# Layer 1's state-space scan in half-chunk steps with two channel groups

## The chip, the core and the metric

The kernel runs on one core of a Trainium2 chip. Its engines work side by side: TensorE (PE in the profile, with its weight loads as PEld), VectorE (DVE), ScalarE (ACT), GpSimd (POOL) and SyncE (SP), which issues most of the DMA transfers. The metric is the time of one execution on the device, in microseconds, as the median of several runs. Everything is in fp32.

## What is computed

Four layers follow one another on an image of 2 x 64 channels x 96 x 96. Layer 0 is attention over the 9216 positions, layer 1 a small convolution and one state-space block ("Mamba"), layer 2 four such blocks (two directions along each of two axes), and layer 3 a dynamic 3 x 3 filter. The change touches the state-space block of layer 1. Cut to what matters:

```python
def _mamba(h, ...):                        # h: (batch, L = 9216, 64)
    ...                                    # projections, short convolution: xc, z (batch, L, 128)
    dt = softplus(dt @ dt_proj_w.T + dt_proj_b)       # (batch, L, 128)
    A = -exp(A_log)                                   # (128, 16)
    dA  = exp(dt[..., None] * A)                      # decay, per channel and state
    dBx = dt[..., None] * Bm[:, :, None, :] * xc[..., None]
    def step(hc, inp):
        dA_t, dBx_t, C_t = inp
        hc = hc * dA_t + dBx_t                        # the recurrence along L
        y = einsum('bds,bs->bd', hc, C_t)
        return hc, y
    _, ys = lax.scan(step, zeros, ...)
    ys = (ys + xc * Dp) * silu(z)
    return einsum('bld,cd->blc', ys, out_proj_w)
```

In layer 1 the recurrence runs over all 9216 positions of an image. In layer 2 it runs over single rows or columns of 96 positions and starts at zero in each.

## The kernel before

The sequence is cut into chunks of `CH = 768` positions, 12 to an image. A unit is one chunk: layer 1 has 24 units, layer 2 has 96. The 128 channels x 16 states are 2048 recurrences; 128 partitions hold 8 channels x 16 states, so a unit has 16 groups of 8 channels. For each unit, `dt` and `dt * xc` are written to DRAM and read back so that every channel's row lands on 16 partitions (the tile `spread`).

Layer 1 takes one channel group over the whole chunk in a step (768 columns). Layer 2 (`u.paired`) takes two channel groups over half a chunk, `HALF = 384` columns each, so it also has 16 steps of 768 columns; its sequences begin inside a chunk, where the decay is made zero, and one scan can run across both groups.

```python
def paired(self, step):
    half, m = divmod(step, self.STEPS // 2)
    return half, (2 * m, 2 * m + 1)

def read(self, u, step):                            # DMA: spread <- rows
    u.dtu[step] = self.work("spread", 2 * CH, bufs=6)
    if not u.paired:
        self.nc.sync.dma_start(out=u.dtu[step], in_=u.rows[8 * step : 8 * step + P])
        return
    half, groups = self.paired(step)
    for q, n in enumerate(groups):
        row = u.rows[8 * n : 8 * n + P, bass.ts(half, CH)]
        self.nc.sync.dma_start(out=u.dtu[step][:, bass.ts(q, CH)], in_=row)

def decay(self, u, step):                           # ScalarE: h = exp(rate * dt)
    h = u.h[step] = self.work("h", bufs=9)
    if not u.paired:
        self.nc.scalar.activation(h, u.dtu[step][:, :CH], AF.Exp, scale=u.w.rates[:, step : step + 1])
        return
    for q, n in enumerate(self.paired(step)[1]):
        dt = u.dtu[step][:, q * CH : q * CH + HALF]
        self.nc.scalar.activation(h[:, bass.ts(q, HALF)], dt, AF.Exp, scale=u.w.rates[:, n : n + 1])

def shared(self, u, half=0):                        # TensorE: B of the unit, into PSUM
    if u.paired:
        sides, halves = [self.low[0]], [half]
    else:
        (sides, u.B), halves = self.places[1], range(2)
    for j, p in zip(halves, sides):
        self.nc.tensor.matmul(p, lhsT=u.w.bc[0], rhs=u.xc[:, bass.ts(j, HALF)], start=True, stop=True)

def inputs(self, u, step):                          # VectorE: the product dt*x*B, into PSUM
    if not u.paired:
        u.bx = self.places[0][1]
        self.nc.vector.tensor_mul(u.bx, u.dtu[step][:, CH:], u.B)
        return
    bx = self.places[step % 2][1].rearrange("p (q t) -> p q t", q=2)
    x = u.dtu[step].rearrange("p (q a t) -> p q a t", q=2, a=2)[:, :, 1]
    B = self.low[0].unsqueeze(1).to_broadcast([P, 2, HALF])
    self.nc.vector.tensor_mul(bx, x, B)

def scan(self, u, step):                            # VectorE: the recurrence; GpSimd: times C
    nc = self.nc
    h = u.h[step]
    if not u.paired:
        first = u.carry[:, step : step + 1]
        nc.vector.tensor_tensor_scan(h, h, u.bx, first, ALU.mult, ALU.add)
        nc.gpsimd.tensor_copy(first, h[:, CH - 1 :])
        nc.gpsimd.tensor_mul(h, h, u.C)
        return
    bx = self.places[step % 2][1]
    way = slice(None, None, -1) if u.rev else slice(None)
    nc.vector.tensor_tensor_scan(h[:, way], h[:, way], bx[:, way], 0.0, ALU.mult, ALU.add)
    ...                                             # GpSimd: h times C, C broadcast over the two groups

def gather(self, u, step):                          # TensorE: sum over the 16 states, into y
    if u.paired:
        half, groups = self.paired(step)
        parts = [(half, self.low[1], q, n) for q, n in enumerate(groups)]
        ...
    else:
        parts = [(j, p, j, step) for j, p in enumerate(self.low)]
        ...
    ...                                             # first the direct term Dp * xc, then two products a step
```

PSUM is used as follows: `places` are two tiles of 768 columns, `low` two of 384. In layer 1 `places[0]` holds the product, `places[1]` holds B, and `low` the two halves of y. In layer 2 both `places` hold products in turn, `low[0]` holds B and `low[1]` y, each for half a chunk.

The order of the steps in the program, the same for all engines (each engine takes its own instructions out of it):

```python
for n in range(begin, len(steps) + end + 1):
    s = n % self.STEPS
    ...                                             # read of step n + 5, decay of step n + 3
    if at(n):
        u = at(n)[0]
        if not u.paired:
            self.inputs(u, s)
        elif s % 2 == 0:
            self.inputs(u, s)
            self.inputs(u, s + 1)
        self.scan(u, s)
        if u.paired and s == 6:
            self.shared(u, 1)
        if s == (14 if u.paired else 15) and unit(n // self.STEPS + 1):
            after = unit(n // self.STEPS + 1)
            if after.paired and not u.paired:       # from layer 1 to layer 2
                for late in (2, 1, 0):
                    self.gather(u, s - late)
                self.y_read(u)
                u.drained = True
            self.shared(after)
    ...                                             # gather of step n - 2; then the pieces of the units to come and past
```

The pieces are the other parts of a unit (norm, convolution, gate, step size, C, the output), spread over the steps of the units before and after; each uses one shared PSUM tile `mm` in turn.

Of the kernel before, what the change touches and what calls it, by code (L numbers as in the profile page):

```python
# [19 lines left out]
FP = mybir.dt.float32  # L20
AF = mybir.ActivationFunctionType
ALU = mybir.AluOpType
# [3 lines left out]
P = 128  # L26
B, C, H, W = 2, 64, 96, 96
L = H * W
EPS = 1e-5
NB = 512  # L30

D_STATE, DT_RANK, D_CONV = 16, 4, 4
HALF = 4 * W
CH = 2 * HALF
# [579 lines left out]
class Mamba:  # L614
# [19 lines left out]
    def __init__(self, k, tables, wk, dram, ps, ps_m):  # L634
        self.k, self.nc, self.t = k, k.nc, tables
        self.wk, self.dram, self.ps_m = wk, dram, ps_m


        self.places = [self.wide(ps.tile([P, 2 * NB], FP, name=f"place{i}")) for i in range(2)]
        self.low = [ps.tile([P, NB], FP, name=f"low{i}")[:, :HALF] for i in range(2)]  # L640

    def work(self, tag, n=CH, **kw):
        return self.wk.tile([P, n], FP, tag=tag, name=tag, **kw)
# [138 lines left out]
    def step_read(self, u):  # L782
        nc = self.nc

        u.both = self.work("dtu", 2 * CH, bufs=1)
        order = "p (j a t) -> p a j t" if u.paired else "p (a j t) -> p a j t"
        both = u.both.rearrange(order, a=2, j=2)
        u.dt, u.e = both[:, 0], both[:, 1]
        u.kept = self.by_half(self.work("kept", bufs=1))
        p = self.by_half(u.p)  # L790
        nc.scalar.activation(u.e, p, AF.Abs, bias=u.w.dt_b)
        nc.scalar.activation(u.dt, p, AF.Relu, bias=u.w.dt_b)
# [39 lines left out]

    def paired(self, step):
        half, m = divmod(step, self.STEPS // 2)
        return half, (2 * m, 2 * m + 1)

    def read(self, u, step):
        u.dtu[step] = self.work("spread", 2 * CH, bufs=6)  # L840
        if not u.paired:
            self.nc.sync.dma_start(out=u.dtu[step], in_=u.rows[8 * step : 8 * step + P])
            return
        half, groups = self.paired(step)
        for q, n in enumerate(groups):
            row = u.rows[8 * n : 8 * n + P, bass.ts(half, CH)]
            self.nc.sync.dma_start(out=u.dtu[step][:, bass.ts(q, CH)], in_=row)

    def decay(self, u, step):

        h = u.h[step] = self.work("h", bufs=9)
        if not u.paired:
            self.nc.scalar.activation(h, u.dtu[step][:, :CH], AF.Exp, scale=u.w.rates[:, step : step + 1])  # L853
            return
        for q, n in enumerate(self.paired(step)[1]):
            dt = u.dtu[step][:, q * CH : q * CH + HALF]
            self.nc.scalar.activation(h[:, bass.ts(q, HALF)], dt, AF.Exp, scale=u.w.rates[:, n : n + 1])  # L857

    def shared(self, u, half=0):

        if u.paired:
            sides, halves = [self.low[0]], [half]
        else:
            (sides, u.B), halves = self.places[1], range(2)
        for j, p in zip(halves, sides):
            self.nc.tensor.matmul(p, lhsT=u.w.bc[0], rhs=u.xc[:, bass.ts(j, HALF)], start=True, stop=True)  # L866

    def inputs(self, u, step):

        if not u.paired:  # L870
            u.bx = self.places[0][1]
            self.nc.vector.tensor_mul(u.bx, u.dtu[step][:, CH:], u.B)  # L872
            return
        bx = self.places[step % 2][1].rearrange("p (q t) -> p q t", q=2)
        x = u.dtu[step].rearrange("p (q a t) -> p q a t", q=2, a=2)[:, :, 1]
        B = self.low[0].unsqueeze(1).to_broadcast([P, 2, HALF])
        self.nc.vector.tensor_mul(bx, x, B)  # L877

    def scan(self, u, step):
        nc = self.nc  # L880
        h = u.h[step]
        if not u.paired:
            first = u.carry[:, step : step + 1]
            nc.vector.tensor_tensor_scan(h, h, u.bx, first, ALU.mult, ALU.add)  # L884
            nc.gpsimd.tensor_copy(first, h[:, CH - 1 :])  # L885
            nc.gpsimd.tensor_mul(h, h, u.C)  # L886
            return
        bx = self.places[step % 2][1]
        way = slice(None, None, -1) if u.rev else slice(None)
        nc.vector.tensor_tensor_scan(h[:, way], h[:, way], bx[:, way], 0.0, ALU.mult, ALU.add)  # L890
        h = h.rearrange("p (q t) -> p q t", q=2)
        C = u.C[:, bass.ts(self.paired(step)[0], HALF)]
        nc.gpsimd.tensor_mul(h, h, C.unsqueeze(1).to_broadcast([P, 2, HALF]))  # L893

    def gather(self, u, step):

        if u.paired:
            half, groups = self.paired(step)
            parts = [(half, self.low[1], q, n) for q, n in enumerate(groups)]
            begin, end = step % 8 == 0, step % 8 == 7  # L900
        else:
            parts = [(j, p, j, step) for j, p in enumerate(self.low)]
            begin, end = step == 0, step == self.STEPS - 1
        h = u.h[step]
        if begin:
            for half, p in {half: p for half, p, _, _ in parts}.items():
                self.nc.tensor.matmul(p, lhsT=u.w.direct, rhs=u.xc[:, bass.ts(half, HALF)], start=True, stop=False)  # L907
        for i, (_, p, q, n) in enumerate(parts):
            stop = end and (i == 1 or not u.paired)
            self.nc.tensor.matmul(p, lhsT=self.t.gather[n], rhs=h[:, bass.ts(q, HALF)], start=False, stop=stop)  # L910

    def y_half(self, u):
        if u.paired:
            u.y = self.work("yg")
            self.nc.scalar.copy(u.y[:, :HALF], self.low[1])  # L915

    def y_read(self, u):
        if u.paired:
            self.nc.scalar.copy(u.y[:, HALF:], self.low[1])
        elif not u.drained:  # L920
            u.y = self.work("yg")
            for j, p in enumerate(self.low):
                self.nc.scalar.copy(u.y[:, bass.ts(j, HALF)], p)

    def y_gate(self, u):
        self.nc.gpsimd.tensor_mul(u.y, u.y, u.gate)
# [60 lines left out]
    OTHER = (3, 5)  # L987

    @staticmethod
    def lates(now, s):  # L990
        halves = now and now[0].paired
        if s == 2 or (s == 10 and halves):
            return ()
        if s == 3 or (s == 11 and halves):
            return (3, 2)
        return (2,)

    def run(self, units, first, n_first, other):


        for u in units:
            u.dtu, u.h, u.paired, u.drained = {}, {}, not u.carry, False
        steps = [(u, s) for u in units for s in range(self.STEPS)]
        at = lambda n: steps[n] if 0 <= n < len(steps) else None
        reads = ("norm_square", "norm_root", "conv_read", "gate_read", "step_read", "c_read", "tail_read")

        table = [[] for _ in range(self.STEPS)]
        unit = lambda i: units[i] if i < len(units) else None
        for offset, name in self.PIECES:
            table[offset % self.STEPS].append((name not in reads, offset, name))  # L1010
        begin, end = self.PIECES[0][0], self.PIECES[-1][0]
# [13 lines left out]
        for n in range(begin, len(steps) + end + 1):  # L1025
            s = n % self.STEPS
            if at(n + self.READ):
                self.read(*at(n + self.READ))
            if at(n + self.DECAY):
                self.decay(*at(n + self.DECAY))  # L1030
            if at(n):
                u = at(n)[0]


                if not u.paired:
                    self.inputs(u, s)
                elif s % 2 == 0:
                    self.inputs(u, s)
                    self.inputs(u, s + 1)
                self.scan(u, s)  # L1040
                if u.paired and s == 6:
                    self.shared(u, 1)
                if s == (14 if u.paired else 15) and unit(n // self.STEPS + 1):
                    after = unit(n // self.STEPS + 1)
                    if after.paired and not u.paired:

                        for late in (2, 1, 0):
                            self.gather(u, s - late)
                        self.y_read(u)
                        u.drained = True  # L1050
                    self.shared(after)
            if n == -1:
                self.shared(units[0])

            for late in self.lates(at(n), s):
                if at(n - late) and not (at(n - late)[0].drained):
                    self.gather(*at(n - late))
            for late in (False, True):
                for is_late, offset, name in table[s]:
                    i = (n - offset) // self.STEPS  # L1060
                    if is_late == late and (0 if n >= 0 else 1) <= i < len(units):
                        getattr(self, name)(units[i])
                if s in self.OTHER and n >= 0 and not late:
                    next(other, None)
# [289 lines left out]
```

## Time and profile before

| | |
|---|---|
| median of 3 runs | 8185.35 us (8180.19 to 8186.09) |
| profiled execution, span | 8174.9 us |
| TensorE (PE) busy | 7554.5 us, 92% |
| VectorE (DVE) busy | 6785.6 us, 83% |
| ScalarE (ACT) busy | 5045.4 us, 62% |
| GpSimd (POOL) busy | 4755.1 us, 58% |
| DMA | 1725.90 MB, mean 211 GB/s |
| layer 1's products and scans | from 2752.4 to 3937.1 us |
| layer 2's products and scans | from 3942.3 to 8093.4 us |

A busy share is a mean over four layers with different limits, so it has to be read by stage. In lists of instructions, `L884` is a line of the kernel, "out<-in" names the tiles, "x2" says that two like instructions are merged into one line, and a bracket at the end gives the engine's idle time ahead of the instruction and what ended it. The clock is the share of its full speed that TensorE was granted.

### The profile page before, as it was taken

How to read it: one execution, taken by the hardware profiler on the slowest of the kernel's cores; microseconds unless marked ns; L12 is line 12 of the kernel's file. 1: busy time of each engine (PE TensorE's matmuls, PEld its weight loads, DVE VectorE, ACT ScalarE, POOL GpSimd, SP SyncE). 2: the span in 40 equal slices, each digit the busy share in tenths (PEclk: the TensorE clock that was granted, in tenths of full speed). 3: DMA queues.
4: the chain of work that ended last, by engine and by line, in shares of the span. 5: the costliest groups of instructions: out<-in, count | busy, mean ns of one | idle time of the engine just before them, and what ended most of it. 6: DMA issues, size and time to landing. Idle time of an engine off the chain costs nothing.

```text
span 8174.9 us, 80364 instructions
## 1 busy us (share of the span) xinstructions
PE 7554.5 (92%) x24578; PEld 3358.0 (41%) x24578; DVE 6785.6 (83%) x5136; ACT 5045.4 (62%) x6473; POOL 4755.1 (58%) x3146
## 2 busy tenths in 40 slices
PE   9999999999999799999889998989999999999897
PEld 3333333333333344444444444444444444444443
DVE  6666666666666599988899999999999999999999
ACT  4444444444444566665676677777777777777774
POOL 0000000000000588888888888898999989888895
PEclk9999999999999798988999999999999999999999
DMA  1000000000000588777888888888898888888885
GB/s 42 1 1 1 1 1 1 3 4 4 4 4 5 205 294 296 284 286 277 292 315 317 317 321 333 330 324 331 334 337 328 330 336 336 331 321 334 324 329 211
DMA packets 538496, 1725.90 MB, mean 211 GB/s; under 512 B 59844, under 2 KB 60996, under 8 KB 537544
## 3 DMA queue, kind: packets, MB, share of 16 engines
q1 hardware_dynamic: 536608, 1717.66, 56.8%
q8 instruction: 194, 3.18, 0.2%
q10 hardware_dynamic: 1448, 3.05, 0.1%
q14 instruction: 246, 2.02, 0.1%
HBM read 1522.68 MB, written 197.79 MB: 210 GB/s over the span
## 4 chain that ended last, share of the span: by engine, by line
PE 21%; POOL 13%; issue 12%; ACT 8%; DMA 8%; DVE 4%; SPq 0%; DVEq 0%; ACTq 0%; POOLq 0%
PE low L910 10%; DMA spread<-rows 6%; POOL h L886 5%; POOL h L893 4%; PE mm L666 4%; ACT h L857 4%; PE conv L754 4%; DVE place L877 2%; DMA rows<-dtu 1%; PE low L907 1%; PE conv L748 1%; DVE h L890 1%; POOL dtu L811 1%; PE low L866 1%; ACT raw L773 1%
## 5 line engine op out<-in xcount | busy, mean ns | idle before, releaser
L910 PE MATMUL low<-h,pair 128*128 128x384 f32 x7680 | 2865.4, 515 | 44.2 <-POOL h L886 26.5
L893 POOL TENSOR_TENSOR h<-h,C 128x768 f32<-128x768 f32 x1536 | 2755.1, 1819 | 231.7 <-DVE h L890 225.1
L890 DVE TENSOR_TENSOR_SCAN h<-h,place 128x768 f32<-128x768 f32 x1536 | 2604.3, 1737 | 4.9 <-ACT h L857 4.9
L910 PEld LDWEIGHTS low<-h,pair 128*128 128x128 f32 x7680 | 1503.2, 201 | 1288.6 <-issue 270.7
L307 ACT ACTIVATE e<-f_exp 128x1536 f32<-128x1536 f32 x864 | 1207.1, 1449 | 1223.7 <-PE f_exp L297 1223.7
L363 DVE TENSOR_TENSOR acc_e<-acc_e,e 128x1536 f32<-128x1536 f32 x792 | 1389.9, 1755 | 684.5 <-ACT e L307 645.2
L857 ACT ACTIVATE h<-spread,xa 128x384 f32<-128x384 f32 x3072 | 1717.2, 607 | 368.7 <-DMA spread<-rows 336.8
L877 DVE TENSOR_TENSOR place<-spread,low 128x768 f32<-128x768 f32 x1536 | 1388.3, 949 | 251.0 <-PE low L866 238.4
L336 POOL TENSOR_TENSOR xa<-xa,t_att 64x512 f32<-64x512 f32 x36 | 45.4, 1261 | 2612.4 <-ACT t_att L334 2612.4
L314 PE MATMUL y_att<-e,xb 128*64 128x512 f32 x5184 | 1243.6, 601 | 0.0
L297 PE MATMUL f_exp<-theta,phi 64*128 64x512 f32 x5184 | 1234.4, 606 | 1.0 <-DVE xb L280 0.5
L297 PEld LDWEIGHTS f_exp<-theta,phi 64*128 64x128 f32 x5184 | 466.2, 186 | 754.6 <-issue 460.8
L884 DVE TENSOR_TENSOR_SCAN h<-h,state,place 128x768 f32<-128x768 f32 x384 | 696.1, 1813 | 67.7 <-ACT h L853 19.2
L886 POOL TENSOR_TENSOR h<-h,C 128x768 f32<-128x768 f32 x384 | 695.3, 1811 | 31.4 <-POOL state L885 1.0
L314 PEld LDWEIGHTS y_att<-e,xb 128*64 128x64 f32 x5184 | 341.5, 136 | 830.7 <-issue 829.3
L765 ACT ACTIVATE raw<-conv,cols 128x768 f32<-128x768 f32 x120 | 108.2, 901 | 886.1 <-PE conv L754 587.0
L754 PE MATMUL conv<-xn,xa 64*128 64x384 f32 (+3 forms) x1536 | 557.9, 503 | 16.6 <-DVE xa L1128 5.3
L872 DVE TENSOR_TENSOR place<-spread,place 128x768 f32<-128x768 f32 x384 | 369.1, 961 | 129.3 <-PE place L866 116.9
L853 ACT ACTIVATE h<-spread,rates 128x768 f32<-128x768 f32 x384 | 351.1, 931 | 175.0 <-DMA spread<-rows 173.6
L907 PE MATMUL low<-raw,xa 128*128 128x384 f32 x384 | 220.2, 662 | 257.8 <-ACT yg L915 175.6
L754 PEld LDWEIGHTS conv<-xn,xa 64*128 64x128 f32 x1536 | 277.6, 190 | 286.7 <-issue 98.7
L805 POOL TENSOR_TENSOR kept<-dtu,kept 128x768 f32<-128x768 f32 x120 | 218.2, 1819 | 285.1 <-ACT kept L798 285.1
(207 smaller groups left out, 6041.4 us busy)
## 6 DMA issues: line engine op xcount, KB each, us to landing
spread<-rows SPq DMA_DIRECT2D x3072, 384.0 KB, 6.4
spread<-rows SPq DMA_DIRECT2D x384, 768.0 KB, 4.5
rows<-dtu SPq DMA_DIRECT2D x240, 768.0 KB, 5.8
image<-pre SPq DMA_DIRECT2D x11, 384.0 KB, 2.3
xb<-image SPq DMA_DIRECT2D x11, 384.0 KB, 7.9
xa<-in_x SPq DMA_DIRECT2D x1, 2304.0 KB, 22.2
out<-xa ACTq DMA_DIRECT2D x7, 240.0 KB, 2.0
out<-xa SPq DMA_DIRECT2D x1, 1200.0 KB
```

The source lines that it names most:

```text
L297: nc.tensor.matmul(fs[j // 3][:, bass.ts(j % 3, NB)], lhsT=phi[at, bass.ts(m // 2, P)], rhs=theta[at, bass.ts(i, NB)], start=True, stop=True,)
L307: nc.scalar.activation(e, f, AF.Exp)
L314: nc.tensor.matmul(y[rows_of(m % 2)], lhsT=g[:, m, :], rhs=es[j // 3][:, bass.ts(j % 3, NB)], start=m < 2, stop=m >= KEYS - 2,)
L363: nc.vector.tensor_add(acc, acc, e)
L754: self.nc.tensor.matmul(p3[:, :, o], lhsT=lhsT, rhs=x3[:, :, i], **flags)
L857: self.nc.scalar.activation(h[:, bass.ts(q, HALF)], dt, AF.Exp, scale=u.w.rates[:, n : n + 1])
L877: self.nc.vector.tensor_mul(bx, x, B)
L884: nc.vector.tensor_tensor_scan(h, h, u.bx, first, ALU.mult, ALU.add)
L886: nc.gpsimd.tensor_mul(h, h, u.C)
L890: nc.vector.tensor_tensor_scan(h[:, way], h[:, way], bx[:, way], 0.0, ALU.mult, ALU.add)
L893: nc.gpsimd.tensor_mul(h, h, C.unsqueeze(1).to_broadcast([P, 2, HALF]))
L910: self.nc.tensor.matmul(p, lhsT=self.t.gather[n], rhs=h[:, bass.ts(q, HALF)], start=False, stop=stop)
```

## The change

Layer 1 now uses the steps of layer 2: two channel groups over half a chunk. Its recurrence carries over from chunk to chunk, so one scan can't run across both groups; each step has two scans of 384 columns, each starting from the state that its group had after the half chunk before. The product of the next step comes ahead of the scans, into the other of two PSUM tiles, so that no scan has to wait for the product right in front of it and no product for the scan right in front of it. With one form of step, the branches for the two kinds and the drain between the layers go, and `low` becomes `B` and `y`.

```diff
-        self.low = [ps.tile([P, NB], FP, name=f"low{i}")[:, :HALF] for i in range(2)]
+        self.B, self.y = [ps.tile([P, NB], FP, name=name)[:, :HALF] for name in ("B", "y")]
...
     def read(self, u, step):
+        half, turns = self.turns(step)
         u.dtu[step] = self.work("spread", 2 * CH, bufs=6)
-        if not u.paired:
-            self.nc.sync.dma_start(out=u.dtu[step], in_=u.rows[8 * step : 8 * step + P])
-            return
-        half, groups = self.paired(step)
-        for q, n in enumerate(groups):
+        for q, n in enumerate(turns):
...
     def decay(self, u, step):
 
         h = u.h[step] = self.work("h", bufs=9)
-        if not u.paired:
-            self.nc.scalar.activation(h, u.dtu[step][:, :CH], AF.Exp, scale=u.w.rates[:, step : step + 1])
-            return
-        for q, n in enumerate(self.paired(step)[1]):
+        for q, n in enumerate(self.turns(step)[1]):
...
     def scan(self, u, step):
         nc = self.nc
-        h = u.h[step]
-        if not u.paired:
-            first = u.carry[:, step : step + 1]
-            nc.vector.tensor_tensor_scan(h, h, u.bx, first, ALU.mult, ALU.add)
-            nc.gpsimd.tensor_copy(first, h[:, CH - 1 :])
-            nc.gpsimd.tensor_mul(h, h, u.C)
-            return
...
+        half, turns = self.turns(step)
+        h, bx = u.h[step], self.places[step % 2][1]
+        h2 = h.rearrange("p (q t) -> p q t", q=2)
+        if u.carry:
+            state = u.carry[:, turns[0] : turns[1] + 1]
+            for q in range(2):
+                at = bass.ts(q, HALF)
+                nc.vector.tensor_tensor_scan(h[:, at], h[:, at], bx[:, at], state[:, q : q + 1], ALU.mult, ALU.add)
+            nc.gpsimd.tensor_copy(state.unsqueeze(2), h2[:, :, HALF - 1 :])
+        else:
+            way = slice(None, None, -1) if u.rev else slice(None)
+            nc.vector.tensor_tensor_scan(h[:, way], h[:, way], bx[:, way], 0.0, ALU.mult, ALU.add)
+        nc.gpsimd.tensor_mul(h2, h2, u.C[:, bass.ts(half, HALF)].unsqueeze(1).to_broadcast([P, 2, HALF]))
...
-                if not u.paired:
-                    self.inputs(u, s)
-                elif s % 2 == 0:
+                if s % 2 == 0:
                     self.inputs(u, s)
                     self.inputs(u, s + 1)
                 self.scan(u, s)
-                if u.paired and s == 6:
+                if s == 6:
                     self.shared(u, 1)
-                if s == (14 if u.paired else 15) and unit(n // self.STEPS + 1):
-                    after = unit(n // self.STEPS + 1)
-                    if after.paired and not u.paired:
-
-                        for late in (2, 1, 0):
-                            self.gather(u, s - late)
-                        self.y_read(u)
-                        u.drained = True
-                    self.shared(after)
+                if s == 14 and at(n + 2):
+                    self.shared(at(n + 2)[0], 0)
...
```

The other edits (`shared`, `inputs`, `gather`, `y_half`, `y_read`, `lates`) take the same branch out: what layer 2 did is now done for both layers.

## The prediction

> **What bounds the kernel now.** I read the page's busy shares first, then its costliest groups, then busy time by stage, then VectorE's instructions in order of time. The changed code runs only in layer 1, so the first thing to find is its stretch. The first product of layer 1 starts at 2752.4 us and the first product of layer 2 at 3942.3 us. Layer 1 is thus 1190 us of 8175, 14.5%; it is 24 units (two images of 12 chunks) of 16 steps, 49.6 us a unit. The rest of the kernel should stay as it is.
>
> These are the groups of VectorE (DVE) in the two layers, from the page; columns are line, operation, shapes and count, then busy us and mean ns of one, then idle time before them:
>
> ```profile
> L890 DVE TENSOR_TENSOR_SCAN h<-h,place 128x768 f32<-128x768 f32 x1536 | 2604.3, 1737 | 4.9 <-ACT h L857 4.9
> L877 DVE TENSOR_TENSOR place<-spread,low 128x768 f32<-128x768 f32 x1536 | 1388.3, 949 | 251.0 <-PE low L866 238.4
> L884 DVE TENSOR_TENSOR_SCAN h<-h,state,place 128x768 f32<-128x768 f32 x384 | 696.1, 1813 | 67.7 <-ACT h L853 19.2
> L886 POOL TENSOR_TENSOR h<-h,C 128x768 f32<-128x768 f32 x384 | 695.3, 1811 | 31.4 <-POOL state L885 1.0
> L872 DVE TENSOR_TENSOR place<-spread,place 128x768 f32<-128x768 f32 x384 | 369.1, 961 | 129.3 <-PE place L866 116.9
> ```
>
> A layer 1 step is one product (L872) and one scan (L884). Next, VectorE in order of time, layer 1 first: start, duration, what ran.
>
> ```profile
> 3195.37 0.96 DVE L872 TENSOR_TENSOR place<-spread,place 128x768 f32<-128x768 f32 x1
> 3196.43 1.81 DVE L884 TENSOR_TENSOR_SCAN h<-h,state,place 128x768 f32<-128x768 f32 x1
> 3198.28 0.96 DVE L872 TENSOR_TENSOR place<-spread,place 128x768 f32<-128x768 f32 x1
> 3199.38 1.81 DVE L884 TENSOR_TENSOR_SCAN h<-h,state,place 128x768 f32<-128x768 f32 x1
> 3201.11 0.26 DVE L589 TENSOR_TENSOR xa<-mats,mm 128x128 f32<-128x128 f32 x1
> ```
>
> Then layer 2, where two products run ahead of two scans:
>
> ```profile
> 5218.57 1.80 DVE L877 TENSOR_TENSOR place<-spread,low 128x768 f32<-128x768 f32 x2
> 5220.28 3.39 DVE L890 TENSOR_TENSOR_SCAN h<-h,place 128x768 f32<-128x768 f32 x2
> 5224.93 1.83 DVE L877 TENSOR_TENSOR place<-spread,low 128x768 f32<-128x768 f32 x2 [1.25 <-PE low L866]
> 5226.66 3.39 DVE L890 TENSOR_TENSOR_SCAN h<-h,place 128x768 f32<-128x768 f32 x2
> 5229.97 1.80 DVE L877 TENSOR_TENSOR place<-spread,low 128x768 f32<-128x768 f32 x2
> ```
>
> The reader is to see starts, not durations. In layer 1 the scan starts 1.06 to 1.10 us after a product of 0.96 us, because it reads what that product just wrote; the next product starts 1.85 us after the scan, because it overwrites what the scan reads. One step is 1.09 + 1.85 = 2.94 us, and 16 of them are 47.1 of the 49.6 us of a unit. VectorE is the bound of layer 1, in a chain with itself. In layer 2, two products take 1.71 us from start to start (5218.57 to 5220.28) and two scans 3.31 us (5226.66 to 5229.97), so two steps take 5.02 us, 2.51 each: shorter than the sum of the durations, since an instruction that doesn't need the one in front of it starts before that one ends. Layer 2 has its own bubble: the product waits 1.25 us for B from TensorE.
>
> Last, busy time by stage; after the engines come the granted TensorE clock, the DMA share and GB/s. The first line is layer 1, the second layer 2, the third a late part of layer 1:
>
> ```profile
> 2752.00:3942.00 1190.00, 1092.31 (x2819) 517.00 (x2819) 1075.57 (x799) 746.30 (x866) 1008.50 (x932) 0.91 0.78 286
> 3942.00:8104.00 4162.00, 3754.31 (x10355) 1911.01 (x10353) 3896.39 (x3109) 2983.18 (x4600) 3683.77 (x2154) 0.95 0.88 326
> 3844.00:3892.00 48.00, 43.36 (x103) 20.78 (x102) 41.35 (x32) 24.86 (x27) 38.17 (x36) 0.82 0.77 278
> ```
>
> TensorE, VectorE and GpSimd are all busy 85 to 92% of layer 1. Where the clock is 0.82, VectorE has gaps of 1.8 us for B and 2.7 us for a decay from ScalarE in each unit, and a unit takes about 50 us: there TensorE is the bound.
>
> [...]
>
> **The change, part by part.**
> *Products.* Two run ahead of the scans they feed. From layer 2: 1.71 us for two from start to start. Before they took 2 × 1.09 = 2.18.
> *Scans.* Each 768-column scan becomes two of 384, each with its own carried state. The length's part: 3.31/2 = 1.655 us for 768 columns[...]. [...] A state read from a column costs more: 3199.38 to 3201.11 is 1.73 us to an instruction that doesn't need the scan, 0.075 more than layer 2's 1.655, and the durations differ by the same (1813 against 1737 ns). [...] Four of them are 3.72 us; two old scans took 2 × 1.85 = 3.70. So splitting eats what the lost wait between scan and product would have given.
> *A pair of steps* is then 1.71 + 3.72 = 5.43 us, against 5.88. A unit's steps: 8 × 5.43 = 43.4 us, against 47.1. Gain 3.7 us a unit, × 24 = 88 us.
> *B.* It is now fetched for each half chunk from one PSUM tile, as in layer 2, where the products waited 238.4 us for it over 96 units, 2.5 a unit. Layer 1 waited 116.9 in all, but 88.0 of that is the wait before the very first product; 28.9 is left, 1.2 a unit. I take 2.5 after the change: 1.3 × 24 = 31 us lost.
> *End of layer 1.* The drain before layer 2 cost one wait of 5.2 us; about 4 us of it go.
> *Beside the path.* The decays become two of 607 ns for one of 931: 16 × 0.28 = 4.5 us more a unit by durations, on an engine busy 746 of 1190 us. GpSimd copies two state columns and not one, at about the 0.18 us of now: per unit 16 × (1.81 + 0.18) plus five products of 1.81 and one of 1.54 are 42.4 us, under 46. The carried state is read eight steps after it is written, not sixteen; that is still over 20 us. Reads become two of 384 KB for one of 768 KB, which layer 2 sustains at 2.7 us a step. TensorE's work is the same; layer 1 asks it for 2819 / 24 = 117 passes a unit, and at 384 columns, 320 ns at full clock (an estimate: the 0.344 us from pass to pass in this layer times the clock of 0.93 there), that is 37.5 us, 41 us at 0.91 and 46 us at 0.82.
> *Sum.* 88 − 31 + 4 = 61 us. A unit goes from 49.6 to about 47.2 us, layer 1 to about 1130. I take 1 us off this gain for units at 0.82, whose cost is mostly in the 49.6 us of now. 8185 − 60 = 8125 us, 0.7% less.
>
> **Rivals.**
> *TensorE becomes the bound.* For: 41 us of passes in 47 us, two waits per unit for the y tile where there was one, and a clock that fell to 0.82 in the last 190 us of layer 1. [...] Against: layer 2 runs 2.49 passes per us at 0.95, layer 1 now 2.37 at 0.91. If it holds for all of layer 1, the time stays at 8175 to 8190.
> *The split scan costs more than 0.93.* If a scan with a carried state can't start before the scan in front of it has ended, each costs its full duration, 0.93 + 0.08: four cost 0.32 more a pair, 2.6 us a unit, 61 us. The gain is then gone: 8186. Against: in 3201.11 an instruction did start 0.08 us before such a scan ended.
> *The state's read is hidden behind the scan in front.* Then a half scan costs 0.855, a pair 5.13, and the gain rises by 8 × 0.3 × 24 = 58 us, to 8067. I see nothing that speaks for it but the overlap of other instructions.
> *GpSimd's lag.* Five long operations in nine steps, each making it late by 1.8 us, could hold h. Nine buffers of h are there, three more steps than one lives; layer 2 bears the same pattern. I give it 10 to 20 us at the worst.
>
> **Range and chances.** The working point is 8125. The rivals against move it to 8175 or 8186, the one for it to 8067, none of them likelier than one in six; half of B's wait gone or doubled moves it by 30. So 8085 to 8165 in 8 of 10. A gain over 2% needs 164 us, 14% of layer 1, beyond even the best rival; a loss of that size needs units of 56 us, for which I see no cause. Chances 0.02, 0.96, 0.02.
>
> **What would show it.** Right: in layer 1, two products start to start 1.7 us, the scans 0.93 us apart, a pair 5.43; waits for B about 2.5 us a unit; layer 1 about 1130 us; layer 2 and the attention unchanged. Wrong: scans a full duration apart or with a semaphore between them; VectorE's idle time before the scan growing, released by ScalarE's decays or GpSimd's state; a clock in layer 1 well below 0.91; or waits for B of 4 us a unit and more.

## The result and the profile after

| | before | after |
|---|---|---|
| median | 8185.72 us (4 runs) | 8052.01 us (8041.52 to 8060.9, 4 runs) |
| ratio | | 0.9836, 95% interval 0.9819 to 0.9853 |
| span of the profiled execution | 8174.9 us | 8039.6 us |
| layer 1, first product to layer 2's first | 1189.8 us, 49.58 a unit | 1070.6 us, 44.61 a unit |
| layer 2, to layer 3's first instruction on VectorE | 4162.2 us | 4146.1 us |
| TensorE's clock in layer 1 | 0.91 | 0.98 |
| of it at half clock | 214 us | 44 us |

The change took 134 us off. The prediction had 60, and the measured time lies below its range. In the profiles 119 us of the gain are in layer 1.

VectorE's groups on the page after (line, what, count, then busy us and mean ns, then idle time before them):

```profile
L874 DVE TENSOR_TENSOR_SCAN h<-h,place 128x768 f32<-128x768 f32 x1536 | 2604.1, 1736 | 4.9 <-ACT h L849 4.9
L859 DVE TENSOR_TENSOR place<-spread,B 128x768 f32<-128x768 f32 x1920 | 1736.3, 948 | 345.3 <-PE B L853 326.3
...
L870 DVE TENSOR_TENSOR_SCAN h<-h,state,place 128x384 f32<-128x384 f32 x768 | 714.2, 991 | 0.0
```

The scan of layer 1 (L870) now has 0.0 us of idle time ahead of it, where it had 67.7. Each is 991 ns long, which is not what it costs; for that, VectorE in order of time in layer 1:

```profile
3205.59 1.80 DVE L859 TENSOR_TENSOR place<-spread,B 128x768 f32<-128x768 f32 x2
3207.30 3.72 DVE L870 TENSOR_TENSOR_SCAN h<-h,state,place 128x384 f32<-128x384 f32 x4
3210.94 1.80 DVE L859 TENSOR_TENSOR place<-spread,B 128x768 f32<-128x768 f32 x2
3212.65 3.72 DVE L870 TENSOR_TENSOR_SCAN h<-h,state,place 128x384 f32<-128x384 f32 x4
```

Two products take 1.71 us from start to start, four half scans 3.64, a pair of steps 5.35 us (5.88 before). A half scan is thus 0.91 us.

VectorE's waits for B (total, times, longest), in layer 1 after its first product, then in layer 2:

```profile
DVE place L859 <- PE B L853: 27.8, 20, 2.8
DVE place L859 <- PE B L853: 210.9, 94, 4.3
```

That is 1.16 us a unit in layer 1, as before the change (28.9 us, 1.2 a unit), and 2.20 in layer 2.

Busy time by stage, layer 1 and then layer 2, columns as in the prediction (engines, clock, DMA share, GB/s):

```profile
2752.00:3823.00 1071.00, 991.69 (x2806) 485.08 (x2806) 1041.10 (x1183) 813.17 (x1244) 997.99 (x930) 0.98 0.86 316
3823.00:7969.00 4146.00, 3742.74 (x10371) 1907.03 (x10369) 3897.94 (x3110) 2990.18 (x4608) 3689.62 (x2158) 0.95 0.88 328
```

VectorE is busy for 97% of layer 1 (90% before). TensorE's matmuls are the same in number, but run at a clock of 0.98 in place of 0.91. The prediction allowed for a lower clock in layer 1, and not for a higher one.

**What the clock of 0.91 was.** The prediction read means over 48 us, and took 0.82 for a steady value. These are TensorE's busy time, clock, DMA share and GB/s in layer 1 of the kernel before, in windows of 3.41 us laid so that the clock changes at their edges:

```profile
3195.12:3198.54 3.42, 2.58 (x7) 1.00 0.77 282
3198.54:3201.95 3.41, 1.07 (x4) 1.00 0.75 268
3201.95:3205.37 3.42, 3.42 (x7) 0.50 0.83 271
3205.37:3208.78 3.41, 3.41 (x6) 0.50 0.82 283
3208.78:3212.19 3.41, 3.41 (x10) 1.00 0.12 49
```

And TensorE's instructions there:

```profile
3201.42 5.00 PE L748 MATMUL conv<-xn,taps 64*128 64x384 f32 x8 [2.34 <-DVE xa L589]
3206.35 2.74 PE L910 MATMUL low<-h,pair 128*128 128x384 f32 x4
3209.02 2.85 PE L748 MATMUL conv<-xn,taps 64*128 64x384 f32 x8
```

The clock is whole or half (1.00 or 0.50). It halves right after a window in which TensorE was busy only 1.07 of 3.41 us, here because it waited 2.34 us for VectorE to read a PSUM tile. Eight passes of the convolution then take 5.00 us, and 2.85 us a little later. In layer 1 the clock halves about once a unit, 23 times, each time after a window with 0.37 to 2.17 us of matmuls; but windows with 1.56 us were also followed by whole clock, so these traces give no threshold. Half clock lasts one to five windows. One of five:

```profile
3249.74:3266.81 17.07, 17.07 (x25) 0.50 0.74 267
```

A mean of 0.82 is 36% of the time at half clock; over all of layer 1 the trace has 214 us of it before and 44 after. None of the 23 windows ahead of a halving was wholly idle, and in the stretch of 17.07 us TensorE was busy through five windows at half clock. What ends the half clock is not shown.

### The profile page after: what moved, and what is told of

It reads as the page before. It is cut to its first block, busy times and chain, and to the rows that moved or that the text cites. A ratio compares the mean times of both kernels' runs of the same rounds, so it can differ in the third digit from the quotient of the medians.

```text
span 8039.6 us, 82139 instructions
## 1 busy us (share of the span) xinstructions
PE 7441.1 (93%) x24578; PEld 3321.5 (41%) x24578; DVE 6752.5 (84%) x5520; ACT 5118.4 (64%) x6857; POOL 4749.0 (59%) x3146
## 4 chain that ended last, share of the span: by engine, by line
PE 19%; issue 9%; ACT 8%; DMA 7%; POOL 5%; DVE 4%; SPq 0%; DVEq 0%; ACTq 0%; POOLq 0%
PE y L884 10%; DMA spread<-rows 5%; PE conv L752 4%; POOL h L875 4%; ACT h L849 4%; PE mm L664 3%; DVE place L859 2%; PE y L881 1%; DMA rows<-dtu 1%; PE B L853 1%; DVE h L874 1%; ACT raw L771 1%; DVE xa L1207 1%; POOL dtu L808 1%; ACT L772 1%
## 5 line engine op out<-in xcount | busy, mean ns | idle before, releaser
L884 PE MATMUL y<-h,pair 128*128 128x384 f32 x7680 | 2805.0, 508 | 14.0 <-POOL h L875 10.6
L859 DVE TENSOR_TENSOR place<-spread,B 128x768 f32<-128x768 f32 x1920 | 1736.3, 948 | 345.3 <-PE B L853 326.3
L884 PEld LDWEIGHTS y<-h,pair 128*128 128x128 f32 x7680 | 1499.7, 199 | 1192.3 <-issue 216.9
L870 DVE TENSOR_TENSOR_SCAN h<-h,state,place 128x384 f32<-128x384 f32 x768 | 714.2, 991 | 0.0
L849 ACT ACTIVATE h<-spread,rates 128x384 f32<-128x384 f32 x768 | 425.9, 607 | 57.5 <-DMA spread<-rows 51.4
L881 PE MATMUL y<-raw,xa 128*128 128x384 f32 x384 | 216.7, 652 | 261.2 <-ACT yg L888 175.3
L664 PE MATMUL mm<-raw,xa 128*128 128x384 f32 x768 | 279.5, 487 | 0.9 <-ACT xb L920 0.7
L881 PEld LDWEIGHTS y<-raw,xa 128*128 128x128 f32 x384 | 68.0, 222 | 398.5 <-ACT yg L888 206.1
```

The costliest lines, as they stand in the source:

```text
L664: self.nc.tensor.matmul(o, lhsT=lhsT, rhs=x, start=n == 0, stop=n == len(terms) - 1)
L859: self.nc.vector.tensor_mul(bx, x, self.B.unsqueeze(1).to_broadcast([P, 2, HALF]))
L870: nc.vector.tensor_tensor_scan(h[:, at], h[:, at], bx[:, at], state[:, q : q + 1], ALU.mult, ALU.add)
L884: self.nc.tensor.matmul(self.y, lhsT=self.t.gather[n], rhs=rhs, start=False, stop=stop)
```

## The experiments

Three theories. **A**: the gain is VectorE's shorter chain alone. **B**: a second part comes from TensorE's clock: where its gaps are shorter it halves less often, and B and the decays come in time. **C**: the new order of B, y and gathers by half chunk raises the clock. Ratios are against the kernel before, measured beside each.

### Taking the product ahead away again

```diff
-                if s % 2 == 0:
+                if u.carry and s % 8 < 6:
+                    self.inputs(u, s)
+                elif s % 2 == 0:
                     self.inputs(u, s)
                     self.inputs(u, s + 1)
```

> The kernel after the change, but in layer 1's steps 0 to 5 and 8 to 13 of a unit each product stands right in front of its two scans (steps 6, 7, 14 and 15 keep two products ahead, so B is fetched at the same points as after). A step without the product ahead should take 1.09 us to its scans plus two half scans of 0.91, 2.91 in place of 2.67 us; over 12 steps that is 2.8 us a unit, 68 us in all. Theory A (VectorE's chain alone): 8052 + 68 = 8120 us, TensorE's clock in layer 1 stays near 0.98. Theory B (pace: where VectorE's steps are longer, TensorE has longer gaps and its clock halves more often, and this gives the loss a second part): clock back to 0.93 or less and 8140 to 8180 us. Rival C (the order of B, y and the gathers by half chunk is what raised the clock): clock stays at 0.97 or more, as A.

Measured: 8116.41 us, ratio 0.9917 (0.9893 to 0.9940); layer 1 is 1138.9 us, 47.46 a unit. VectorE in order of time:

```profile
3198.04 0.94 DVE L859 TENSOR_TENSOR place<-spread,B 128x768 f32<-128x768 f32 x1
3199.12 1.92 DVE L870 TENSOR_TENSOR_SCAN h<-h,state,place 128x384 f32<-128x384 f32 x2
3200.95 0.94 DVE L859 TENSOR_TENSOR place<-spread,B 128x768 f32<-128x768 f32 x1
```

A step is 2.91 us (3198.04 to 3200.95), and a unit 2.85 us longer than after, the 2.8 that was worked out. So the product ahead is worth 0.24 us a step, and the split scans by themselves cost nothing against the one scan (2.91 against 2.94 us). The time is what A says, but the clock is as none of the three expected: 0.94, with 141 us at half clock, between the 44 of the change and the 214 of the kernel before. The waits for B stayed at 25.2 us and those for decays at 3.4: with VectorE slower, a lower clock cost nothing here.

### One scan for two

```diff
-            for q in range(2):
-                at = bass.ts(q, HALF)
-                nc.vector.tensor_tensor_scan(h[:, at], h[:, at], bx[:, at], state[:, q : q + 1], ALU.mult, ALU.add)
+            nc.vector.tensor_tensor_scan(h, h, bx, 0.0, ALU.mult, ALU.add)
```

This leaves out the states that layer 1 carries from one half chunk to the next.

> The kernel after the change, with one scan of 768 columns from zero in layer 1 in place of two with carried states. It leaves the carried states out, so layer 1 computes something else; everything around stays. A pair of steps goes from 5.35 to 5.02 us, 2.6 us a unit, 64 us. If VectorE bounds layer 1 alone: 8052 - 64 = 7988 us. If TensorE takes over, layer 1 goes no faster than layer 2's 43.2 us a unit: 1.4 x 24 = 34 us, 8018 us, with the waits for B above 2 us a unit.

Measured: 8059.75 us, ratio 0.9843 (0.9817 to 0.9869), as fast as the change itself and slower than both expectations. Layer 1 is 1069.8 us, 44.57 a unit, where the change has 44.61. A pair of steps is 5.02 us as expected, 2.6 us a unit less than after, but none of it arrives. VectorE's waits in layer 1 of this kernel (total, times, longest):

```profile
DVE place L859 <- PE B L853: 57.0, 24, 4.2
DVE place L859 <- DMA spread<-rows: 18.5, 19, 1.8
```

At the pace of layer 2's steps, layer 1 has waits for B like layer 2's: 2.37 us a unit against 2.20, where the change has 1.16. Another 0.77 us a unit are waits for the reads of `spread`, of which the change has none in layer 1. So what VectorE saves in its steps it waits for, about half of it at B and a third at these reads. The prediction had carried 2.5 us from layer 2 to a stretch whose steps are 0.16 us longer, 2.6 us over the sixteen of a unit.

### Added work for TensorE in layer 1

If half clock is the cost, work for nothing in TensorE's gaps must make the kernel before faster. The first try put it into PSUM columns next to B:

```diff
+        self.places, self.spare = [self.wide(t) for t in tiles], tiles[1][:, :P]
...
+            self.nc.tensor.matmul(self.spare, lhsT=self.k.ident, rhs=self.k.ident, start=True, stop=True)
...
+            if at(n) and at(n)[0].carry and 1 <= s <= 5:
+                self.fill(4)
```

> The kernel before, with four matmuls of 128 columns added in each of steps 1 to 5 of a unit in layer 1, on the identity into a part of PSUM that nobody reads (about 4 us of TensorE time a unit). Nothing else moves. Theory B (gaps in TensorE's work in the light steps halve its clock): the clock of layer 1 rises from 0.91 to 0.97 or more, the waits for B and for decays shrink, and a unit falls from 49.6 toward the 47.1 of its steps plus about 1.2: 30 to 45 us in all, 8140 to 8155. Theory A or C (the clock has other causes, or its waits cost nothing): clock stays, and the time stays at 8185 or grows by the added work.

Measured: 8189.05 us, ratio 1.0013 (1.0003 to 1.0023). The clock of layer 1 rose to 0.97 and the scans' waits for decays fell from 19.2 to 2.0 us, but VectorE's products now waited 37.4 us on semaphores for the added matmuls, which write into B's tile. Layer 1 took 1198 us. It shows the cause of the half clock, and not its price. The second try adds zeros to y, in a tile that no product reads:

```diff
...
+            self.nc.tensor.matmul(self.low[0], lhsT=self.zero.to_broadcast([P, P]), rhs=u.xc[:, :HALF], start=False, stop=False)
...
+            if at(n) and at(n)[0].carry and 3 <= s <= 5:
+                self.fill(at(n)[0], 2)
```

> The kernel before, with two matmuls of 384 columns by a zero weight added into y's open sum in each of layer 1's steps 3, 4 and 5 (about 3.8 us of TensorE time a unit; y is unchanged, and no product of VectorE reads that bank, so nothing waits for the added work itself, unlike in the fill before). Theory B: the clock of layer 1 rises from 0.91 to 0.97 or more, the scans' waits for decays (19 us) go and the waits for B (29 us) fall by half: layer 1 20 to 35 us shorter, 8140 to 8160 us for the kernel. If the half clock in layer 1 costs nothing, or its waits stay: 8175 to 8190.

Measured: 8130.41 us, ratio 0.9940 (0.9927 to 0.9953), a larger gain than expected. First VectorE's waits in layer 1 of the kernel before:

```profile
DVE place L872 <- PE place L866: 116.9, 18, 88.0
DVE h L884 <- ACT h L853: 19.2, 12, 2.9
DVE place L877 <- PE low L866: 5.2, 1, 5.2
```

then those with the added work:

```profile
DVE place L878 <- PE place L872: 90.0, 6, 87.4
DVE place L883 <- PE low L872: 4.6, 1, 4.6
DVE h L890 <- DVE place L878: 1.0, 2, 0.5
```

and its stages (layer 1, layer 2):

```profile
2751.00:3898.00 1147.00, 1087.02 (x3109) 533.71 (x3109) 1075.76 (x800) 749.98 (x866) 1009.01 (x932) 0.99 0.81 297
3898.00:8060.00 4162.00, 3752.06 (x10354) 1909.33 (x10352) 3896.62 (x3110) 2983.15 (x4601) 3686.39 (x2155) 0.95 0.88 326
```

Without the wait before the first product (88.0 and 87.4 us), the waits for B fell from 28.9 to 2.6 us and those for decays from 19.2 to none. Layer 1 went from 1189.8 to 1146.5 us, 43 us shorter with 290 more passes on TensorE, and layer 2 stayed at 4162.2. So half clock in layer 1 had cost the kernel before about 43 us.

### Added work for TensorE in both layers, after the change

```diff
...
+        self.spare = tiles[0][:, HALF:]
...
+            if at(n) and s in (2, 3, 4, 10):
+                self.fill(4)
```

> The kernel after, with four such matmuls in each of steps 2, 3, 4 and 10 of every unit of both layers, into the free end of B's bank (about 3.4 us of TensorE time a unit). In layer 2 TensorE runs at half clock for 386 us, most of it right after it waited for y's copy by ScalarE or for C. Theory B: the clock of layer 2 rises from 0.95 to 0.98 or more, the products' waits for B (about 2.1 us a unit) halve, and the time falls by 80 to 120 us, to 7930 to 7970. If the gap itself and not the clock makes TensorE late, or the added work costs as much as it gives: 8050 or more.

Measured: 8400.05 us, ratio 1.0262 (1.0235 to 1.0289). VectorE's waits in both layers name the reason; L841 is the added matmul, in the unused end of B's tile:

```profile
DVE place L865 <- PE B L841: 551.8, 183, 8.2
DVE place L865 <- PE B L859: 51.9, 72, 2.3
```

The added matmuls in turn waited 101.5 us for these products. The clock of layer 2 did rise, to 0.97, but the fault of the first fill, larger here, hides what it is worth.

### Where layer 2's half clock comes from

In layer 2, TensorE waits for ScalarE's copy of y's first half. TensorE in the kernel after:

```profile
5043.75 2.85 PE L884 MATMUL y<-h,pair 128*128 128x384 f32 x8
5050.30 1.65 PE L881 MATMUL y<-raw,xa 128*128 128x384 f32 x2 [3.70 <-ACT yg L888]
```

The first edit brings the copy forward:

```diff
         self.nc.scalar.activation(u.raw, u.raw, AF.Silu)
+        if self.due:
+            self.y_half(self.due)
+            self.due = None
         self.nc.scalar.preload_act_table_set("natural_log_exp_and_others")
...
```

> The kernel after, with ScalarE's copy of y's first half moved ahead of the table load that follows the gate's Silu (it stood behind that load and a step's decays). The copy comes about 2 us sooner. If TensorE's wait for this copy is what halves its clock and makes B late in layer 2: the wait (346 us in all before this edit) falls by half, the clock of layer 2 rises from 0.95 to 0.97 or more, the waits for B fall from 2.2 to about 1 us a unit, and the time falls by 60 to 120 us, to 7930 to 7990. If B is late for another reason: TensorE waits elsewhere and the time stays at 8040 to 8060.

The 346 us add up the waits of the weight loads (186.5) and of the matmuls behind them (159.4), and so count one wait twice.

Measured: 8012.92 us, ratio 0.9798 (0.9784 to 0.9811), between the two expectations. Layer 2 is 4117.2 us, and its waits for B fell from 210.9 to 88.9 us; but ScalarE now waits for TensorE at the copy (123.3 us, 13.4 before this edit), the scans wait 94.2 us for decays (4.9), and the clock is 0.96. The second edit leaves the copy and fills the gap, in the units that have no output to compute:

```diff
...
+            if s == 10 and at(n) and n >= 26 and not units[(n - 26) // self.STEPS].last:
+                self.fill(self.open()[0][0], at(n)[0], 4, True)
```

> The kernel after, with four matmuls of 384 columns by a zero weight into an unread tile, only in those units of layer 2 in which TensorE has no output to compute in steps 9 and 10 and waits up to 4 us for y's copy (47 of 96 units, 2.6 us each). The gap stays, but TensorE works in it. If the half clock after the gap makes B late (theory B for layer 2): layer 2's clock rises to 0.97 or more, waits for B fall from 211 to about 110 us, 7940 to 7980 us in all. If the gap itself makes B late, not the clock: waits for B and time as after, 8040 to 8060, or more by the added work.

Measured: 7991.65 us (7977.69 to 8006.92), ratio 0.9771 (0.9746 to 0.9796), the fastest of all. TensorE at the gap, then layer 2 as a whole:

```profile
5035.07 2.74 PE L841 MATMUL mm<-raw,zero 128*128 128x384 f32 x8
5038.94 0.91 PE L887 MATMUL y<-raw,xa 128*128 128x384 f32 x2 [1.12 <-ACT yg L894]
```

```profile
3828.00:7921.00 4093.00, 3794.51 (x10755) 1945.17 (x10753) 3898.97 (x3110) 2992.53 (x4607) 3689.35 (x2158) 0.97 0.88 332
```

The trace has the added matmuls in 48 units. The gap is as long as it was, but the two passes behind it take 0.91 us and not 1.65. The clock went to 0.97, the time at half clock from 386 to 215 us, the waits for B from 210.9 to 154.3 us, layer 2 from 4146 to 4093 us. So a part of what makes B late in layer 2 is the half clock and not the gap, as B says; the gain of 60 us is below the 72 to 112 that were expected.

Two combinations. The earlier copy with the zero sum of layer 1 (as in the second try above, steps 3 to 5):

> The kernel with y's copy moved ahead of the table load, and in layer 1 two matmuls of 384 columns by a zero weight added to y's open sum in each of steps 3, 4 and 5. Layer 1's clock is 0.98 already and its waits for B are 24 us in all. If the rest of these waits comes from the clock: layer 1 falls from 1063 to about 1045 us, 7995 us for the kernel. If TensorE is simply full there (112 passes and more in 44 us): the added 3.8 us a unit make B later, layer 1 grows to 1080 us or more and the kernel to 8030.

Measured: 8044.71 us, ratio 0.9835 (0.9816 to 0.9855). Layer 1 grew from 1068.5 us (the 1063 of the expectation ends two steps early) to 1105.5 us at a clock of 0.99, with waits for B of 54.6 us. The work that took 43 us off the kernel before adds 37 us here: there is little half clock left in layer 1 to remove (39 us before this fill, 24 with it), and the added passes make B later. And the two edits for layer 2 together, with two added matmuls a unit:

> The kernel after with both: y's copy ahead of the table load, and two matmuls by a zero weight in step 10 of layer 2's units that have no output to compute. Each edit alone took 39 and 60 us off. If they mend different parts of layer 2's half clock, 7950 to 7970 us; if both mend the same wait, the earlier copy leaves little gap to fill: 7990 to 8015.

Measured: 8013.56 us, ratio 0.9792 (0.9775 to 0.9808). No better than the earlier copy alone, and with its waits for decays (101.3 us); that fits two edits that work on the same wait.

## Why the prediction was wrong, step by step

- **VectorE as the bound of layer 1, products ahead at 1.71 us a pair**: right to the digit, and the first experiment gave the 2.91 us step that its terms make.
- **Half scan 0.93 us**: 0.91. The 0.93 was the author's estimate; the traces before show 1.655 us for 768 columns from a constant and 0.075 more with a state from a column, but no scan of 384. A pair is 5.35 and not 5.43 us. But the step of 2.94 us was a little long for the kernel before: its mean without waits is 2.92, and 2.68 after. So the steps gave 93 us, where the prediction had 88.
- **B: "I take 2.5 after the change"**: this is the step that failed. It was 1.16 us a unit, as before (1.2), so the 31 us of loss never came. One scan for two has 2.37 us at layer 2's pace: the wait is what is left when TensorE's way to B is set against VectorE's steps, and can't be carried from one pace to another. Whether B's waits would have grown without the rise of the clock is not shown.
- **The clock: "I take 1 us off"**: failed too, and with it the 19.2 us of waits for decays, which the prediction left as they were and which went. A mean of 0.82 was read as a steady limit that the change would keep. It was half clock after gaps. That it had a price, these 19 us among it, is shown by the fill (43 us). Why the change has so little of it is shown only in part. With VectorE's steps made longer again, half clock rises from 44 to 141 us, so pace matters; but it doesn't reach 214, and the scans wait 3.4 us for decays, not 19.2. The rest may come from the new order of the matmuls (C) or from the decays in halves, which were not separated.
- **End of layer 1**: 4 us expected; the 5.2 us wait is gone.
- **Sum**: where VectorE's time in layer 1 goes, in us; its work is summed from start to start, without the waits of more than 0.15 us:

| | work | waits for B | for decays | other waits | layer 1 | at half clock |
|---|---|---|---|---|---|---|
| before | 1135.1 | 28.9 | 19.2 | 6.7 | 1189.8 | 214 |
| after | 1041.3 | 27.8 | 0 | 1.5 | 1070.6 | 44 |
| no product ahead | 1109.3 | 25.2 | 3.4 | 1.0 | 1138.9 | 141 |
| one scan for two | 985.6 | 57.0 | 0 | 27.2 | 1069.8 | 40 |
| before, zeros added to y | 1137.8 | 2.6 | 0 | 6.1 | 1146.5 | 14 |

The change's 119 us are 94 of work, 19 of waits for decays, 5 at the end and 1 at B, where the prediction had 88, 0, 4 and a loss of 31. The 43 us of the fill are no share of these 119: it removes waits for B too, which the change keeps, and on top of the change with the earlier copy it adds 37.

- **Layer 2 "stays as it is"**: it came out 16 us shorter with the same steps. Among the profiles with these steps and nothing added to layer 2, its length goes roughly with its time at half clock: 4146 us with 386 (after), 4154 with 406 and 4170 with 434 (the first two experiments), 4162 with 420 (before) and with 413 (zeros added to y), 4175 with 440 (the first fill). What sets that time is open, so this part of the gain is not claimed for the change.
- **Rivals**: full durations for carried states (1.01 us a half scan) and the hidden state read (0.855) are not seen at the 0.91 measured, nor is GpSimd's lag: after the change VectorE waits for nothing from GpSimd in layer 1. "TensorE becomes the bound" is about where the change has arrived: less work for VectorE gives nothing, more work for TensorE costs 1.5 us a unit.

## What to carry to other kernels

Read a clock below 1 in windows as short as its steps before treating it as a limit: the mean of 0.91 here was whole clock with 214 us of half clock after gaps, and 44 us were left when VectorE's steps were shorter. A wait between two engines is a difference of two paths, so it is worked out anew for the new pace and not copied from another stage (B's was 1.16 us a unit at 5.35 us a pair and 2.37 at 5.02). And when the bound engine leads by only a few per cent, as VectorE did here (it waited 55 of layer 1's 1190 us), look for the point where the next engine takes over: here 2.6 us a unit less for VectorE gave nothing after the change.

## What was not expected of the hardware

- The clock halved after a 3.41 us window with 1.07 us of matmuls in it, and stayed half for up to 17.07 us while TensorE was busy throughout. Twelve passes a unit of multiplications by zero (some 3.9 us, an estimate from the 2.58 us that eight passes of 384 columns take at a clock of 1.00 in layer 2 before, 5217.63 to 5220.21) left 14 of layer 1's 214 us at half clock: 8130.41 us against 8176.77 for the kernel before beside it.
- A scan of 384 columns with a state read from a column costs 0.91 us behind another such scan, though each is 0.99 us long; 768 columns from a constant cost 1.655. So the split costs 0.16 us for 768 columns.
- In these programs VectorE's reads of a PSUM tile waited on semaphores for matmuls into other, unread columns of it: 551.8 us. The waits are the program's; whether the chip needs them is not shown.
